# Layer 3 of a four-layer model: the four scan directions summed with tokens on the partitions, with D * x and layer norm done there, and group norm's deviation moved to ScalarE

## The chip, the cores and the metric

The kernel runs on one core of one Trainium2 chip, in float32. The metric is device microseconds from the first to the last instruction of one launch that computes all four layers for 16 images of 192 channels and 32 x 32 pixels.

## The reference, cut to what matters

Each layer adds its output to its input, after a group norm of 32 groups:

```python
x = x + _L0(_gn(x), ...)     # an mLSTM block and a 3x3 convolution
x = x + _L1(_gn(x), ...)     # a Mamba block
x = x + _L2(_gn(x), ...)     # a depthwise convolution and a batch norm
x = x + _L3(_gn(x), ...)     # a Mamba block that scans the image in four directions

def _gn(v, G=32, eps=1e-5):  # mean and variance over a group's channels and pixels
    return ((g - m) / jnp.sqrt(s + eps)).reshape(v.shape)
```

What the change touches in layer 3 (DI = 384, 16 states, L = 32 * 32 tokens):

```python
x_in, z = (xz[:, :DI], xz[:, DI:])
xc = silu(_dwconv(x_in, conv_w, conv_b, ((1, 2), (1, 2))))
x_hw, x_wh = rows_in_order(xc), columns_in_order(xc)
xs = stack([x_hw, x_wh, x_hw[..., ::-1], x_wh[..., ::-1]])     # four directions
def step(h, inp):                                              # for each direction
    h = h * exp(dt_t[..., None] * A) + (dt_t * u_t)[..., None] * B_t
    y = sum(h * C_t, axis=-1)
ys = scan(step) + Ds * xs
y = ys[0] + inv_wh(ys[1]) + ys[2][..., ::-1] + inv_wh(ys[3][..., ::-1])
y = (y - mean(y)) / sqrt(var(y) + 1e-5) * ln_g + ln_b          # over the 384 channels
y = y * silu(z)
g_out = y @ W_out + b_out
return wts[0] * g_out + wts[1] * l_out                         # l_out: a convolution branch
```

`inv_wh` turns a sequence that ran down the columns back into row order.

## The kernel before, in words

Layer 0 works in chunks of 128 tokens; layers 1 and 2 run together; layer 3 has a loop of its own, `scan_run`. The pieces are tied together by queues written out by hand: `Side` holds generators with a start and an end, counted in steps, and `tick` runs each one's share of pieces between the pieces of the main loop. A scheduler then settles the order on each engine, and every engine takes its instructions strictly in order.

A **step** of layer 3 is one of 16 states of one **unit**, and a unit is one direction over one half (512 tokens) of one image, so an image has 8 units and 128 steps. The directions come in the order k = 0, 2 (rows, forward and backward), then 1, 3 (columns). In a step ScalarE computes three decays (`da`, L986) and scales three inputs (`xbt`, L966); TensorE turns the inputs so that channels lie on partitions (`xb`, L994 and L997); VectorE runs three scans of 128x512 (`h`, L1010); GpSimd multiplies all three by C (L1017, one instruction of 128x1536; a small `carry` copy, L1016, in every other unit); and TensorE adds the result to `y` in PSUM, turned so that tokens lie on partitions (L1028), two steps later. `y` has a single buffer: when a unit's sixteenth state is in, `layer3_sum` reads it out (L1466 by ScalarE for the first direction of a pair, L1468 by VectorE to add the second), and the next unit's first L1028 waits for that. SyncE's queue loads a row of C per step (`cb`, L968).

Everything else of an image is side work at fixed steps `at` (counted from the image's first):

- steps 2 to 8: `layer3_columns` of the image before. Six blocks of four transposes (L1064) bring the sum of the two column directions back to channels on partitions, and VectorE adds each to `v` with a strided pattern (L1490).
- steps 8 to 36: `layer3_tail` of the image before. For each half, layer norm over the channels, which lie on partitions: matmuls with a matrix of 1/384 for mean and variance (L377, L385), differences and products by VectorE (L379, L389), squares, logarithm and exponential by ScalarE (L384, L386, L387); silu of z between two loads of function tables (L1283, L1284); gain and bias (L1656); the product with silu(z) by GpSimd (L1660). Then the output projection (L1668), and VectorE adds the residual (L1671).
- steps 36.5 to 45: `layer3_front` of the next image, with `group_norm`: statistics by VectorE, a matmul over the groups, epsilon by VectorE (L367), the power -0.5 by GpSimd (L309), then the normalization by VectorE (L1545).
- steps 45 to 78: the next image's convolution branch (`layer3_local`) and z (`layer3_z`, matmuls L1594, whose input is read along the image's rows).
- steps 66 to 74: `layer3_rows`: the sum of the two row directions back to channels on partitions, with D * x (L1477).
- steps 78 to 112: the next image's `layer3_xc` (projection and a 4x4 depthwise convolution, L1171, then silu).
- steps 114 to 125: `prep` of the next image's first unit. Each other unit's `prep` (its dt, B and C rows, L887 to L937) runs 14 to 3 steps before the unit; column units read `xc` with a stride of 32 elements in L887.

After the last step the last image's columns and tail run alone. `group_norm` serves all four layers.

Of the kernel before, what the change touches and what calls it, by code (L numbers as in the profile page):

```python
# [22 lines left out]
W = 32  # L23
# [5 lines left out]
EPS = 1e-5  # L29
# [67 lines left out]
def lay_out(a):  # L97
# [26 lines left out]
    p128.add("3conv_r", taps(a["L3_conv_conv_w"].reshape(DI, 4, 4)))  # L124
    for n in ("b_in", "conv_b", "ln_g", "ln_b"):
        p128.vec("3" + n, a["L3_conv_" + n])
    p128.vec("3Ds", a["L3_conv_Ds"].T)
    p128.vec("3A_log", a["L3_conv_A_log"].transpose(1, 0, 2))

    def in96(w):  # L130
        return w.reshape(2, HP, -1).transpose(1, 0, 2)
# [13 lines left out]
    def x_rows(w):  # L145
# [35 lines left out]
        "w3_dt": pair(dt_rows, a["L3_conv_dt_proj_w"], a["L3_conv_dt_proj_b"]).reshape(-1, 2 * DI),  # L181
        "w3_out": in128(a["L3_conv_W_out"]),
        "w3_pw": in96(a["L3_conv_pw_w"].T),
    }
    arrays = {k: np.ascontiguousarray(v) for k, v in arrays.items()}
    return arrays, p96.at, p128.at, const.at, const0.at
# [88 lines left out]
class Program:  # L275
# [68 lines left out]
    def group_norm(self, pool, psum, x):  # L344

        nc = self.nc
        st = pool.tile([HP, 2, 2, 6], F32, name="gnst")
        mv = pool.tile([HP, 2, 2], F32, name="gnmv")
        for m in range(2):
            for i, h in enumerate(halves()):  # L350
                nc.vector.bn_stats(st[:, m, i], x[:, m, h])
            nc.vector.bn_aggr(mv[:, m], st[:, m].rearrange("p a b -> p (a b)"))
            yield 1
        ps = psum.tile([128, 512], F32, name="mm")
        nc.tensor.matmul(ps[:HP, :2], self.k("group", HP), mv[:, :, 0], start=True, stop=True)
        mean = pool.tile([HP, 2], F32, name="gnmean")
        nc.vector.tensor_copy(mean, ps[:HP, :2])
        d = pool.tile([HP, 2], F32, name="gnd")
        nc.vector.tensor_tensor(d, mv[:, :, 0], mean, SUB)
        q = pool.tile([HP, 2], F32, name="gnq")  # L360
        nc.vector.tensor_tensor(q, d, d, MUL)
        nc.vector.tensor_tensor(q, q, mv[:, :, 1], ADD)
        yield 1
        ps = psum.tile([128, 512], F32, name="mm")
        nc.tensor.matmul(ps[:HP, :2], self.k("group", HP), q, start=True, stop=True)
        r = pool.tile([HP, 2], F32, name="gnr")
        nc.vector.tensor_scalar(r, ps[:HP, :2], EPS, None, ADD)  # L367
        self.pow_mhalf(r)
        yield 1
        return mean, r, d  # L370

# [1005 lines left out]
    def layer3(self):  # L1377
        tc = self.tc
        with (
# [53 lines left out]
            for b in range(self.nb):  # L1433
                at = 8 * NS * b
                if b:
                    side.add("columns", self.layer3_columns(b - 1, bp, psum), at + 2, at + 8)
                    side.add("tail", self.layer3_tail(b - 1, bp, psum), at + 8, at + 36)
                else:
                    side.add("local", self.layer3_local(0, sp, bp, psum), 3, 33)
                    side.add("z", self.layer3_z(0, bp, psum), 5, 35)  # L1440
                for j in range(1, 8):
                    side.add("prep", prep(units[8 * b + j]), at + 16 * j - 14, at + 16 * j - 3)
                if b + 1 < self.nb:
                    side.add("front", self.layer3_front(b + 1, sp, bp, dp, psum), at + 36.5, at + 45)
                    side.add("local", self.layer3_local(b + 1, sp, bp, psum), at + 45, at + 77)
                    side.add("z", self.layer3_z(b + 1, bp, psum), at + 46, at + 78)
                side.add("rows", self.layer3_rows(b, bp, psum), at + 66, at + 74)
                if b + 1 < self.nb:
                    side.add("xc", self.layer3_xc(b + 1, bp, dp, psum), at + 78, at + 112)
                if b + 1 < self.nb:  # L1450
                    side.add("prep", prep(units[8 * b + 8]), at + 114, at + 125)
# [1 line left out]
            finish(self.layer3_xc(0, bp, dp, psum))  # L1453
            finish(prep(units[0]))
            self.scan_run(units, side, bp, psum)
            finish(self.layer3_columns(self.nb - 1, bp, psum))
            finish(self.layer3_tail(self.nb - 1, bp, psum))

    def layer3_sum(self, u, y, bp):

        im = self.image[u.b]
        if u.k < 2 and u.half == 0:
            im["sum"] = bp.tile([128, 8, DI], F32, name="ysum", bufs=1)
        t = im["sum"][:, 4 * u.half : 4 * u.half + 4].rearrange("p c d -> p (c d)")
        if u.k < 2:
            self.nc.scalar.copy(t, y)  # L1466
        else:
            self.nc.vector.tensor_tensor(t, t, y, ADD)  # L1468

    def layer3_rows(self, b, bp, psum):  # L1470

        im = self.image[b]
        v = im["v"] = bp.tile([128, 3, S], F32, name="v", bufs=1)
        for t in range(3):
            for i, h in enumerate(halves()):
                ps = self.untranspose(im["sum"][:, 4 * i : 4 * i + 4], t, psum)
                self.nc.vector.scalar_tensor_tensor(  # L1477
                    v[:, t, h], im["xc"][:, t, h], self.ds[:, t : t + 1], ps, MUL, ADD
                )
                yield  # L1480

    def layer3_columns(self, b, bp, psum):

        im = self.image[b]
        v = im["v"].rearrange("p t (h w) -> p t w h", w=W)
        for t in range(3):
            for i in range(2):
                ps = self.untranspose(im["sum"][:, 4 * i : 4 * i + 4], t, psum)
                o = v[:, t, 16 * i : 16 * i + 16]
                self.nc.vector.tensor_tensor(o, o, ps.rearrange("p (w h) -> p w h", h=W), ADD)  # L1490
                yield

    def layer3_weights(self, wp, bp, dp):
        nc = self.nc
# [10 lines left out]
        self.ds = wp.tile([128, 3], F32, name="ds")  # L1505
        nc.vector.tensor_reduce(self.ds, self.v128("3Ds", 0, 12).rearrange("p (t k) -> p t k", k=4), AX.X, ADD)

        self.t_conv = dp.tile([3, 128, 16, 32], F32, name="t_conv3", bufs=1)
        for t in range(3):
# [77 lines left out]
    def layer3_z(self, b, bp, psum):  # L1587

        nc = self.nc
        for i in range(2):  # L1590
            for t in range(3):
                ps = psum.tile([128, 512], F32, name="mm")
                for m in range(2):
                    nc.tensor.matmul(  # L1594
                        ps, self.w_in[:, m, DI + t * 128 : DI + (t + 1) * 128],
                        self.xpad[:, m, 1 + 16 * i : 17 + 16 * i, 1 : 1 + W], start=m == 0, stop=m == 1,
                    )
                z = bp.tile([128, 512], F32, name="xt")
# [42 lines left out]
        self.silu(xc)  # L1641
        yield

    def layer3_tail(self, b, bp, psum):

        nc = self.nc
        im = self.image.pop(b)
        wts, v = im["wts"], im["v"]
        for i, h in enumerate(halves()):
            sz = bp.tile([128, 3, 512], F32, name="tmp", bufs=1)  # L1650
            nc.sync.dma_start(sz, self.sz3[b % 2, i])
            vs = [v[:, t, h] for t in range(3)]
            yield from self.layer_norm(bp, psum, vs, vs, self.k("ones384"), 128, 512)
            self.silu(sz)
            for t in range(3):
                nc.scalar.activation(  # L1656
                    v[:, t, h], v[:, t, h], AF.Identity, bias=self.v128("3ln_b", t), scale=self.v128("3ln_g", t)
                )
                yield 0.4
            nc.gpsimd.tensor_tensor(v[:, :, h], v[:, :, h], sz, MUL)  # L1660
            yield 0.4
        for m in range(2):
            for h in halves():
                x = bp.tile([HP, 512], F32, name="xt")
                nc.sync.dma_start(x, self.x3[b, :, m, h])
                ps = psum.tile([128, 512], F32, name="mm")
                for t in range(3):
                    nc.tensor.matmul(  # L1668
                        ps[:HP], self.w_out[:, t, m * HP : (m + 1) * HP], v[:, t, h], start=t == 0, stop=t == 2
                    )  # L1670
                nc.vector.scalar_tensor_tensor(x, ps[:HP], wts[:, 0:1], x, MUL, ADD)  # L1671
                nc.sync.dma_start(self.out[b, m * HP : (m + 1) * HP, h], x)
                yield 2.6

    def router(self, sp, psum, d, r):

# [34 lines left out]
```

## Time and profile before

| | us |
|---|---|
| median of 3 runs | 17365.07 (17350.37 to 17365.62) |
| the profiled execution's own time | 17403.5 |
| its span, first to last instruction | 17401.7 |
| layer 3's scan loop, from the first scan to the last | 7767 to 17335 |
| one image of it | 601 to 604 |

| engine | busy us of the span |
|---|---|
| PE (matmul) | 15749.6 (91%) |
| DVE (VectorE) | 13122.0 (75%) |
| ACT (ScalarE) | 11873.6 (68%) |
| POOL (GpSimd) | 11450.8 (66%) |

A group's line gives its source line, engine, operation, tile, shape and count, then the busy time of the group and the mean duration of one in ns. In a table by stretch each number pair is busy us and a count. A matmul of float32 leaves two records, a transpose one. A busy PE includes the time in which a matmul drains.

### The profile page before, as it was taken

The numbers are of one execution on the slowest core, as the hardware profiler recorded it, in microseconds if no ns is written. First come the engines' busy times: TensorE is split into PE (matmuls) and PEld (weight loads), VectorE is DVE, ScalarE is ACT, GpSimd is POOL, SyncE is SP. The second block draws the span as 40 slices with busy tenths as digits, with TensorE's granted clock in tenths as the row PEclk, the third lists the DMA queues.
The fourth block names the chain that finished last, engine by engine and source line by source line (L and its number), as shares of the span: only waits on it lengthen the run. The fifth ranks groups of instructions, "written<-read, shape, count | busy, mean of one in ns | idle before, by whom it ended". The sixth has DMA issues, their size and how long they took to land. (4 is left out here: it accounts for less than half of the span.)

```text
span 17401.7 us, 263068 instructions
## 1 busy us (share of the span) xinstructions
PE 15749.6 (91%) x99452; PEld 11013.2 (63%) x99452; DVE 13122.0 (75%) x14859; ACT 11873.6 (68%) x19637; POOL 11450.8 (66%) x5555
## 2 busy tenths in 40 slices
PE   8998988888988899979899999999999999999998
PEld 4444444435555555547777777777777777777777
DVE  4444444437777777749889888888888888888888
ACT  3222322327666666648888888888888888888888
POOL 3333333425555555538788788888878888888888
PEclk8889998989999999989999999999999999999999
DMA  1111111123333343433333333323333333333332
GB/s 51 42 40 44 44 43 44 47 63 107 114 110 110 113 118 116 118 99 103 90 99 107 93 96 101 107 83 99 107 98 92 99 108 88 96 105 102 88 98 67
DMA packets 890141, 1544.65 MB, mean 89 GB/s; under 512 B 83472, under 2 KB 314653, under 8 KB 879530
## 3 DMA queue, kind: packets, MB, share of 16 engines
q1 hardware_dynamic: 888874, 1527.81, 30.3%
q8 instruction: 788, 12.91, 0.3%
q14 instruction: 479, 3.92, 0.1%
HBM read 1284.22 MB, written 243.27 MB: 88 GB/s over the span
## 5 line engine op out<-in xcount | busy, mean ns | idle before, releaser
L1017 POOL TENSOR_TENSOR h<-h,cb 128x1536 f32<-128x1536 f32 x2560 | 8872.8, 3469 | 1432.0 <-DVE h L1010 902.9
L986 ACT ACTIVATE da<-dt,neg_a 128x512 f32<-128x512 f32 x7680 | 5267.0, 714 | 1752.0 <-DVE h L1010 1687.3
L1010 DVE TENSOR_TENSOR_SCAN h<-da,carry,xb 128x512 f32<-128x512 f32 x3840 | 4652.4, 1262 | 657.1 <-PE xb L997 596.2
L1028 PE MATMUL y<-const,h 128*128 128x128 f32 x30720 | 4717.9, 276 | 128.3 <-DVE ysum L1468 54.0
L1010 DVE TENSOR_TENSOR_SCAN h<-da,xb 128x512 f32<-128x512 f32 x3840 | 4440.6, 1202 | 388.7 <-PE xb L997 270.7
L994 PE MATMUL xb<-const,xbt 128*128 128x128 f32 x23040 | 4074.6, 282 | 422.5 <-DVE h L1010 269.3
L966 ACT ACTIVATE xbt<-ut,bt 128x384 f32<-128x384 f32 x7680 | 4174.4, 603 | 246.4 <-PE xb L994 244.3
L994 PEld LDWEIGHTS xb<-const,xbt 128*128 128x128 f32 x23040 | 2757.2, 143 | 1815.5 <-issue 643.8
L1028 PEld LDWEIGHTS y<-const,h 128*128 128x128 f32 x30720 | 3684.9, 143 | 322.8 <-issue 265.4
L997 PE MATMUL xb<-diag,ut 128*128 128x128 f32 x15360 | 3016.4, 279 | 0.0
L997 PEld LDWEIGHTS xb<-diag,ut 128*128 128x128 f32 x15360 | 2383.5, 195 | 63.1 <-issue 63.1
L830 POOL TENSOR_TENSOR hs<-h,mhm 128x384 f32<-128x384 f32 x128 | 108.5, 848 | 1685.1 <-DVE den L835 1290.5
L1016 POOL COPY carry<-h 128x3 f32<-128x3 f32 x1280 | 250.5, 196 | 1220.1 <-DVE h L1010 964.7
L976 POOL TENSOR_TENSOR diag<-const,bt 128x512 f32<-128x512 f32 x640 | 680.8, 1064 | 550.5 <-PE xb L997 362.1
L705 POOL TENSOR_TENSOR e<-e,const 128x1536 f32<-128x1536 f32 x128 | 439.9, 3437 | 288.9 <-DMA e<-row 273.0
L520 PE MATMUL conv<-ya,w_conv 128*64 128x512 f32 (+1 forms) x1152 | 543.9, 656 | 66.1 <-DMA ya<-yrows 62.2
L916 PE MATMUL mm<-dbl,w_dt 45*128 45x512 f32 x960 | 532.8, 639 | 33.6 <-DVE v L1490 16.2
L711 ACT ACTIVATE e<-e 128x1536 f32<-128x1536 f32 x128 | 189.7, 1482 | 417.7 <-POOL e L706 417.4
L854 DVE TENSOR_TENSOR ht<-sz,mm 128x384 f32<-128x384 f32 x128 | 70.7, 552 | 519.5 <-PE mm L851 519.5
L1171 PE MATMUL mm<-rep,t_dw 96*32 96x512 f32 x2304 | 433.5, 614 | 23.5 <-DMA rep<-xr 17.3
L779 PEld LDWEIGHTS num<-v,p 128*128 128x128 f32 x3072 | 389.3, 201 | 102.2 <-issue 77.9
L920 DVE SCALAR_TENSOR_TENSOR dt<-lnsq,mm 128x512 f32<-128x512 f32 x480 | 322.0, 671 | 171.9 <-ACT lnsq L919 171.9
(272 smaller groups left out, 17910.1 us busy)
## 6 DMA issues: line engine op xcount, KB each, us to landing
cb<-row SPq DMA_DIRECT2D x2560, 256.0 KB
rep<-xr SPq DMA_DIRECT2D x384, 331.0 KB
e<-row SPq DMA_DIRECT2D x128, 768.0 KB
rep<-xin SPq DMA_DIRECT2D x384, 256.0 KB
rep<-xr SPq DMA_DIRECT2D x384, 228.8 KB
x<-x SPq DMA_DIRECT2D x48, 768.0 KB
xr<-xin SPq DMA_DIRECT2D x48, 612.5 KB
xr<-xpad SPq DMA_DIRECT2D x32, 867.0 KB
```

The source lines that it names most:

```text
L520: nc.tensor.matmul(o, self.w_c2[:k, t, c0 : c0 + o.shape[0]], src[:k, r0 : r0 + 16, dx : dx + W], start=t == 0, stop=t == 14, skip_group_c ...
L705: nc.gpsimd.tensor_tensor(k.e, k.e, self.k0("mask")[:, None, :].to_broadcast([128, NH, 128]), ADD)
L916: nc.tensor.matmul(ps, w_dt[:, t * 128 : (t + 1) * 128], dbl, start=True, stop=True)
L966: nc.scalar.activation(t[:, c], u.ut[:, c], AF.Copy, scale=u.bt[:, c, n : n + 1])
L976: nc.gpsimd.tensor_tensor(d, ident[:, None, :].to_broadcast([128, 4, 128]), u.bt[:, 3, n : n + 4][:, :, None].to_broadcast([128, 4, 128]), ...
L986: nc.scalar.activation(da[i, t], u.dt[:, t], AF.Exp, scale=u.neg_a(t, n))
L994: in_order(nc.tensor.transpose(xb[i, t][:, c * 128 : (c + 1) * 128], xbt[i][:, c, t * 128 : (t + 1) * 128], ident))
L997: in_order(nc.tensor.matmul(xb[i, t][:, 384:], u.ut[:, 3, t * 128 : (t + 1) * 128], u.diag[n // 4][:, n % 4], start=True, stop=True, skip_ ...
L1010: nc.vector.tensor_tensor_scan(hv, dv, xv, 0.0 if first else u.carry_in[:, n, t : t + 1], MUL, ADD)
L1017: nc.gpsimd.tensor_tensor(h[i], h[i], u.c.pop(n)[:, None, :].to_broadcast([128, 3, 512]), MUL)
L1028: in_order(nc.tensor.matmul(u.y[:, j], h[i][:, t, c * 128 : (c + 1) * 128], ident, is_transpose=True, start=n == 0 and j % 4 == 0, stop=n ...
L1171: self.nc.tensor.matmul(ps[32 * g : 32 * g + 32], blocks[:, g * side + r], seen, start=r == 0, stop=r == side - 1, skip_group_check=True,)
```

## The change

`layer3_columns`, `layer3_rows` and `layer3_tail` go. In their place:

- `layer3_turn` writes the row directions' sum (tokens on partitions) to DRAM and reads it back in the columns' order into the same tile, in eight DMAs. The column directions are then added to it by VectorE, so that of eight units only the first two are copied by ScalarE.
- `layer3_skip` adds D * x by GpSimd, in two products and two sums of 128x1536, using `xtok`, which by then holds x in the columns' order.
- `layer3_norm` does layer norm along the free dimension: statistics by VectorE, logarithm and exponential of 4 columns by ScalarE, and one VectorE instruction of 128x384 per block of tokens; then the transposes, with gain and bias applied by ScalarE as it reads PSUM, and the product with silu(z) by GpSimd. The second half of an image is done at steps 115 to 127, the first half at steps 2 to 14 of the next image.
- `layer3_out` loads and stores the residual whole, one buffer instead of two, and VectorE writes it in row order with a strided pattern.
- z is computed in the columns' order: its matmuls read their input down the image's columns.
- `group_norm` takes epsilon, logarithm and exponential by ScalarE instead of VectorE's sum and GpSimd's power, in all layers.

```diff
@@ group_norm
-        nc.vector.tensor_scalar(r, ps[:HP, :2], EPS, None, ADD)
-        self.pow_mhalf(r)
+        nc.scalar.activation(r, ps[:HP, :2], AF.Ln, bias=self.k("eps", HP))
+        nc.scalar.activation(r, r, AF.Exp, scale=-0.5)
@@ layer3
-                    side.add("columns", self.layer3_columns(b - 1, bp, psum), at + 2, at + 8)
-                    side.add("tail", self.layer3_tail(b - 1, bp, psum), at + 8, at + 36)
+                    side.add("norm", self.layer3_norm(b - 1, 0, sp, bp, psum), at + 2, at + 14)
+                    side.add("out", self.layer3_out(b - 1, bp, psum), at + 14.5, at + 35)
...
-                side.add("rows", self.layer3_rows(b, bp, psum), at + 66, at + 74)
+                side.add("turn", self.layer3_turn(b, dp), at + 66.5, at + 68)
+                side.add("skip", self.layer3_skip(b, bp), at + 80, at + 110)
+                side.add("norm", self.layer3_norm(b, 1, sp, bp, psum), at + 115, at + 127)
...
-            finish(self.layer3_columns(self.nb - 1, bp, psum))
-            finish(self.layer3_tail(self.nb - 1, bp, psum))
+            finish(self.layer3_norm(self.nb - 1, 0, sp, bp, psum))
+            finish(self.layer3_out(self.nb - 1, bp, psum))
@@ layer3_sum
-        if u.k < 2:
+        if u.k == 0:
             self.nc.scalar.copy(t, y)
         else:
             self.nc.vector.tensor_tensor(t, t, y, ADD)
+    def layer3_turn(self, b, dp):
+        y = self.image[b]["sum"]
+        rows = dp.tile([S, DI], F32, name="yrows", bufs=2)
+        self.nc.sync.dma_start(rows.rearrange("(c p) d -> p c d", p=128), y)
+        yield Wait(0.7)
+        for c in range(8):
+            self.nc.sync.dma_start(y[:, c], rows.rearrange("(h w) d -> w h d", w=W)[4 * c : 4 * c + 4])
...
+    def layer3_skip(self, b, bp):
...
+        for i in range(2):
...
+            nc.gpsimd.tensor_tensor(dx, im["xtok"][:, h], self.ds[:, None, :].to_broadcast([128, 4, DI]), MUL)
+            yield 1
+            nc.gpsimd.tensor_tensor(im["sum"][:, h], im["sum"][:, h], dx, ADD)
+            yield 1
+    def layer3_norm(self, b, i, sp, bp, psum):
...
+        for c in range(4):
+            nc.vector.bn_stats(st[:, c], y[:, c])
+            nc.vector.bn_aggr(mv[:, c], st[:, c])
+            yield 1
+        r = sp.tile([128, 4], F32, name="lnr")
+        nc.scalar.activation(r, mv[:, :, 1], AF.Ln, bias=self.k("eps"))
+        nc.scalar.activation(r, r, AF.Exp, scale=-0.5)
+        yield 1
+        for c in range(4):
+            nc.vector.tensor_scalar(y[:, c], y[:, c], mv[:, c, 0:1], r[:, c : c + 1], SUB, MUL)
+            yield 0.8
+        self.silu(z)
+        yield 3
         for t in range(3):
+            ps = self.untranspose(y, t, psum)
+            nc.scalar.activation(
+                v[:, t], ps, AF.Identity, bias=self.v128("3ln_b", t), scale=self.v128("3ln_g", t)
+            )
+            yield 1.2
+        nc.gpsimd.tensor_tensor(v, v, z, MUL)
+        yield 1
@@ layer3_z
-                        self.xpad[:, m, 1 + 16 * i : 17 + 16 * i, 1 : 1 + W], start=m == 0, stop=m == 1,
+                        self.xpad[:, m, 1 : 1 + W, 1 + 16 * i : 17 + 16 * i].rearrange("p h w -> p w h"),
+                        start=m == 0, stop=m == 1,
                     )
-                z = bp.tile([128, 512], F32, name="xt")
+                z = bp.tile([128, 512], F32, name="z", bufs=1)
@@ layer3_tail -> layer3_out
-            yield from self.layer_norm(bp, psum, vs, vs, self.k("ones384"), 128, 512)
-            self.silu(sz)
...
-            nc.gpsimd.tensor_tensor(v[:, :, h], v[:, :, h], sz, MUL)
...
+            x = bp.tile([HP, S], F32, name="xt", bufs=1)
+            nc.sync.dma_start(x, self.x3[b, :, m])
+            yield Wait(1.5)
+            for i, h in enumerate(halves()):
...
-                nc.vector.scalar_tensor_tensor(x, ps[:HP], wts[:, 0:1], x, MUL, ADD)
-                nc.sync.dma_start(self.out[b, m * HP : (m + 1) * HP, h], x)
+                o = x.rearrange("p (h w) -> p w h", w=W)[:, 16 * i : 16 * i + 16]
+                nc.vector.scalar_tensor_tensor(
+                    o, ps[:HP].rearrange("p (w h) -> p w h", h=W), wts[:, 0:1], o, MUL, ADD
+                )
+                yield 1
+            nc.sync.dma_start(self.out[b, m * HP : (m + 1) * HP], x)
```

More of the change, by code (lines that the diff above doesn't have):

```diff
@@ L126, in lay_out @@
         p128.vec("3" + n, a["L3_conv_" + n])
-    p128.vec("3Ds", a["L3_conv_Ds"].T)
     p128.vec("3A_log", a["L3_conv_A_log"].transpose(1, 0, 2))
@@ L183, in lay_out @@
         "w3_pw": in96(a["L3_conv_pw_w"].T),
+        "d3": a["L3_conv_Ds"].reshape(1, 4 * DI),
     }
@@ L1455, in layer3 @@
             self.scan_run(units, side, bp, psum)
-            finish(self.layer3_columns(self.nb - 1, bp, psum))
-            finish(self.layer3_tail(self.nb - 1, bp, psum))
+            finish(self.layer3_norm(self.nb - 1, 0, sp, bp, psum))
+            finish(self.layer3_out(self.nb - 1, bp, psum))
     def layer3_sum(self, u, y, bp):
         im = self.image[u.b]
-        if u.k < 2 and u.half == 0:
+        if u.k == 0 and u.half == 0:
             im["sum"] = bp.tile([128, 8, DI], F32, name="ysum", bufs=1)
         t = im["sum"][:, 4 * u.half : 4 * u.half + 4].rearrange("p c d -> p (c d)")
-        if u.k < 2:
+        if u.k == 0:
             self.nc.scalar.copy(t, y)
@@ L1468, in layer3_sum @@
             self.nc.vector.tensor_tensor(t, t, y, ADD)
-    def layer3_rows(self, b, bp, psum):
-        im = self.image[b]
-        v = im["v"] = bp.tile([128, 3, S], F32, name="v", bufs=1)
-        for t in range(3):
[L1475 to L1491, printed above, removed]
+    def layer3_turn(self, b, dp):
[5 more added lines that the diff above has]
+            self.nc.sync.dma_start(y[:, c], rows.rearrange("(h w) d -> w h d", w=W)[4 * c : 4 * c + 4])
+            if c % 2:
+                yield 1
@@ new lines, in layer3_skip @@
+    def layer3_skip(self, b, bp):
+        nc = self.nc
+        im = self.image[b]
+        for i in range(2):
+            h = slice(4 * i, 4 * i + 4)
+            dx = bp.tile([128, 3, 512], F32, name="tmp", bufs=1).rearrange("p a b -> p (a b)")
+            dx = dx.rearrange("p (c d) -> p c d", c=4)
+            nc.gpsimd.tensor_tensor(dx, im["xtok"][:, h], self.ds[:, None, :].to_broadcast([128, 4, DI]), MUL)
+            yield 1
+            nc.gpsimd.tensor_tensor(im["sum"][:, h], im["sum"][:, h], dx, ADD)
+            yield 1
@@ new lines, in layer3_norm @@
+    def layer3_norm(self, b, i, sp, bp, psum):
+        nc = self.nc
+        im = self.image[b]
+        if i:
+            im["v"] = bp.tile([128, 3, S], F32, name="v", bufs=1)
+        v = im["v"][:, :, 512 * i : 512 * i + 512]
+        y = im["sum"][:, 4 * i : 4 * i + 4]
+        z = bp.tile([128, 3, 512], F32, name="tmp", bufs=1)
+        nc.sync.dma_start(z, self.sz3[b % 2, i])
+        st = sp.tile([128, 4, 6], F32, name="lnst")
+        mv = sp.tile([128, 4, 2], F32, name="lnmv")
+        for c in range(4):
[11 more added lines that the diff above has]
+        yield 3
+        for t in range(3):
+            ps = self.untranspose(y, t, psum)
[5 more added lines that the diff above has]
+        yield 1
@@ L1503, in layer3_weights @@
         nc.vector.tensor_scalar(self.neg_a, self.neg_a, -1.0, None, MUL)
-        self.ds = wp.tile([128, 3], F32, name="ds")
-        nc.vector.tensor_reduce(self.ds, self.v128("3Ds", 0, 12).rearrange("p (t k) -> p t k", k=4), AX.X, ADD)
+        d = bp.tile([128, 3, 512], F32, name="tmp", bufs=1).rearrange("p a b -> p (a b)")
+        nc.sync.dma_start(d, self.ins["d3"].partition_broadcast(128))
+        self.ds = wp.tile([128, DI], F32, name="ds")
+        nc.vector.tensor_reduce(self.ds, d.rearrange("p (k d) -> p d k", k=4), AX.X, ADD)
         self.t_conv = dp.tile([3, 128, 16, 32], F32, name="t_conv3", bufs=1)
@@ L1642, in layer3_xc, with layer3_out @@
         yield
-    def layer3_tail(self, b, bp, psum):
+    def layer3_out(self, b, bp, psum):
         nc = self.nc
@@ L1648, in layer3_tail @@
         wts, v = im["wts"], im["v"]
[L1649 to L1652, printed above, removed]
-            yield from self.layer_norm(bp, psum, vs, vs, self.k("ones384"), 128, 512)
-            self.silu(sz)
[L1655 to L1661, printed above, removed]
         for m in range(2):
-            for h in halves():
-                x = bp.tile([HP, 512], F32, name="xt")
-                nc.sync.dma_start(x, self.x3[b, :, m, h])
+            x = bp.tile([HP, S], F32, name="xt", bufs=1)
+            nc.sync.dma_start(x, self.x3[b, :, m])
+            yield Wait(1.5)
+            for i, h in enumerate(halves()):
                 ps = psum.tile([128, 512], F32, name="mm")
@@ L1670, in layer3_tail @@
                     )
-                nc.vector.scalar_tensor_tensor(x, ps[:HP], wts[:, 0:1], x, MUL, ADD)
-                nc.sync.dma_start(self.out[b, m * HP : (m + 1) * HP, h], x)
-                yield 2.6
+                o = x.rearrange("p (h w) -> p w h", w=W)[:, 16 * i : 16 * i + 16]
+                nc.vector.scalar_tensor_tensor(
+                    o, ps[:HP].rearrange("p (w h) -> p w h", h=W), wts[:, 0:1], o, MUL, ADD
+                )
+                yield 1
+            nc.sync.dma_start(self.out[b, m * HP : (m + 1) * HP], x)
     def router(self, sp, psum, d, r):
```

## The prediction

> **What bounds the kernel now.** I began with the busy shares and went to the side work's own stretches, since a share is a mean over stages. The image whose loop starts at 11381.8 is cut at steps 2, 14, 36, 46, 80, 112 and 2 (601.1 us in all). The table of windows gives for each stretch its length, then PE, PEld, DVE, ACT and POOL busy:
>
> ```profile
> 11388.50:11454.30 65.80, 57.87 (x408) 46.55 (x407) 56.37 (x58) 53.85 (x93) 48.28 (x28) 0.97 0.25 67
> 11454.30:11562.00 107.70, 94.39 (x656) 74.68 (x657) 92.51 (x90) 98.47 (x160) 90.67 (x38) 0.98 0.28 80
> 11562.00:11610.00 48.00, 37.12 (x261) 33.66 (x260) 46.11 (x48) 36.42 (x63) 37.45 (x22) 0.86 0.27 85
> 11610.00:11777.00 167.00, 162.30 (x1153) 123.83 (x1153) 148.82 (x147) 135.59 (x234) 131.22 (x63) 1.00 0.36 103
> 11777.00:11921.00 144.00, 143.09 (x1123) 108.42 (x1122) 123.93 (x116) 127.64 (x213) 124.62 (x59) 1.00 0.45 136
> 11921.00:11989.60 68.60, 63.51 (x506) 56.54 (x505) 66.27 (x61) 64.24 (x115) 62.16 (x23) 0.98 0.27 77
> ```
>
> Call them A1, A2, B, C, D, E. No engine bounds the image alone. C and D belong to TensorE (97% and 99%); B and E to VectorE (96%, 97%), in E with ScalarE at 94% close behind. In A1 and A2 nothing is above 91%: waits cost there. Who waits in layer 3 (total us, times, longest), and what stands in for the change's costs:
>
> ```profile
> PE mm L1668 <- POOL v L1660: 77.0, 17, 10.3
> PE y L1028 <- DVE ysum L1468: 54.0, 32, 2.7
> PE y L1028 <- ACT ysum L1466: 21.2, 30, 1.1
> PE y L1028 <- POOL h L1017: 16.9, 27, 1.9
> ```
> ```profile
> 11635.40:11641.30 5.90, 5.48 (x6) 0.91 (x6) 1.00 0.62 170
> 11914.80:11917.90 3.10, 2.83 (x6) 0.93 (x6) 1.00 0.06 19
> ```
> ```profile
> L1541 DVE SCALAR_TENSOR_TENSOR x<-tmp,x x64: 656/730/3481, 7651.5 to 16396.7; 96x512 f32<-96x512 f32 x64
> ```
> ```profile
> L377 PE MATMUL mm<-v,const 128*128 128x512 f32 x192 | 90.4, 593 | 0.3 <-DVE v L1490 0.3
> L385 PE MATMUL mm<-lnsq,const 128*128 128x512 f32 x192 | 108.9, 649 | 43.3 <-ACT lnsq L384 22.5 <-ACT xtok L932 20.8
> L1064 PE MATMUL mm<-const,ysum 128*128 128x128 f32 x1152 | 186.2, 287 | 33.7 <-ACT o L1257 18.5 <-DVE dt L920 6.7 <-DVE o L1140 3.8
> ```
>
> The first: the projection stands in TensorE's queue behind GpSimd's product, 4.8 us per image, and all turns behind it. The second is L887 alone, six records reading `xc` by columns (stride 32), then by rows: 5.48 against 2.83, so a strided record costs 0.44 us more. The third: an instruction with two operands in SBUF takes 0.73 us or up to 3.48.
>
> **What the Trainium skill says.** "SBUF — State Buffer", Door 1: The DMA port swizzle, says SBUF is read in lines of 16 bytes and that accesses which go to a new line each time pay; L887 agrees (0.47 to 0.91 us per record). The same page, Who interferes with whom, says that a VectorE instruction with two SBUF inputs, or in a two-port mode such as tensor_scalar from SBUF, and a GpSimd instruction exclude each other for the whole instruction. L1541 agrees, and L379, with one operand in PSUM, stays at 660 to 689 ns. "ScalarE: Activation LUTs", Table sets: the hidden batching unit, has logarithm and exponential in one set; L386 and L387 follow each other with no load between, so the new pairs need none.
>
> **The change part by part**, per image.
>
> *A1 and A2* (173.5 us; PE 152.3, DVE 148.9, ACT 152.3, POOL 139.0). TensorE loses layer norm's matmuls, (90.4+108.9)/16 = 12.5, and 24 transposes of the columns for 12 of the norm: 768 of L1064's 1152 are layer 3's, 186.2x768/1152/16 = 7.8 for 48, so 3.9 less 1.9. PE 137.8. VectorE loses six L1490 (1.135 each, 6.8) and twelve L379/L389 (0.62, 7.5); it gains four statistics of 384 (L351's 0.667x384/512 = 0.5) with their aggregation (0.18), four normalizations (L577's 512 take 0.546 and L1545's 1024 take 0.80, so about 0.48), and four residuals with a strided output (1.135 as L1490 instead of 0.74): 4.6 + 1.6. The four normalizations are tensor_scalar from SBUF, open to GpSimd's lock; L1541's mean of 1.568 against 0.68 unblocked prices it at 0.9 each (0 to 1.7, half a GpSimd product): 3.6. DVE 144.4. ScalarE loses squares (60.2/16 = 3.8), L386/L387 (2.5), L1656 (4.8) and one of two silus (1.28+1.49+1.28 = 4.05), and gains three reads of PSUM (0.68) and two short ones (0.21 as L839): 12.7 less, 139.6. GpSimd loses one product, 3.45. The busiest falls from 152.3 to 144.4; at the present ratio of 1.14 that is 164.5, and the wait for L1660 (4.8) should go, since the norm ends at step 14 and the projection starts 1.5 steps later or more: 160. I take -13 (-8 to -19).
>
> *B.* VectorE's wait for the power, L1545 <- L309, is 23.7 us over the stage, 1.5 per image. ScalarE takes the pair over; the decays queue behind it. -1.5 (-2.5 to +1: L1545 meets GpSimd's lock, 1.7).
>
> *C.* z's 24 records now read down the columns (stride 34): 24x0.44 = +10.6. The rows' 24 transposes go: -3.9. PE 162.3 becomes 169.0, at 1.03 173.9: +7 (+4 to +10). VectorE's six L1477 (4.4) cost nothing now and free nothing. SyncE gets nine DMAs, the first behind VectorE's sum, the reads behind the write; the C rows queue behind them, but are loaded two steps ahead, as beside the eight reads of `xtok` today. z's single buffer waits for its store; the pieces are over two steps apart. 0 for both; without that cover a few us.
>
> *D* (TensorE at 99%). Two sums go from ScalarE to VectorE, and the next unit's L1028 waits 54.0/32 = 1.7 instead of 21.2/30 = 0.7: +2. GpSimd gets four instructions of 3.45, 13.8, and is then busy 138 of 144. In the order of the changed program one stands at step 73 (in C), two side by side at 82, one at 98. Queued behind them are the products by C, and behind those L1028, with all turns. Today's 32 L1660 are such inserts, and L1028's whole wait for GpSimd is 16.9/32 = 0.5 each: +2; the pair (6.9 us against a cover of about one step) may cost more. +5 in all for D (+2 to +13).
>
> *E.* A norm falls in: VectorE +4.6 and 3.6 of lock, ScalarE +6.5 (4.05 silu, 0.4, 2.0), TensorE +1.9, GpSimd +3.45. ScalarE alone comes to 70.7, VectorE to 74.5, against 68.6. +7 (+3 to +10).
>
> *Sum.* A and B occur 15 times in the loop, C, D, E 16 times: 15x(-14.5) + 16x19 = +87.
>
> *The end.* From the last sum (17341.4) to the end the kernel takes 60.3 us. One norm instead of all columns and both halves: sum 1.7, statistics 2.7, pair 0.5, silu with loads 4.05 (normalization beside it), three reads 2.0, product 3.4, then 24 records of projection, 13.5 (18 take 10.4 today; the first six are slower there too), residual 1.1 and store 3.2: 32, with gaps 33. -27 (-20 to -32).
>
> *Layers 0 to 2.* Group norm makes TensorE wait 96.8 us in layer 0 (L377 <- L543, 15 times). ScalarE's pair stands behind L839/L840, which wait for VectorE behind GpSimd's lock, and the normalization then waits for the same GpSimd instructions: only the power's 0.69 goes, 15 times. GpSimd no longer waits in its queue for L367 (143.9 us, 21 times), ScalarE may instead. -15 (-90 to +40).
>
> Net +45 on the profiled 17403.5, whose own run lies 38 over the median. On the median: **17410**.
>
> **The rivals.**
>
> *A's waits are worth more than their share (faster).* The chain silu, L1656, L1660, L1668 halts every engine: for L1668 the longest wait is 10.3. If A falls by 20 to its busiest engine plus 6%, and C, D, E cost TensorE's share only (+6.7, +2, +3), it is 15x(-21.5) + 16x11.7 - 42 = -177: 17190. With C to E as forecast it decides from -17.5 per image in A and B. For it: 21 us of A lie above its busiest engine. Against: E has no engine below 90%. A milder form, with the middle of both sets, gives 17300.
>
> *TensorE alone sets the period (faster).* Then only 12.5+7.8-3.9-10.6 = 5.8 per image counts: -93-42, 17230. Against: PE is at 93% over the image, and B and E are not its own.
>
> *GpSimd and its lock become the bound (slower).* If the two products at 82 are not covered (+13 in D) and each normalization waits half a product (1.7; A -10, E +9): 15x(-11.5) + 16x29 - 42 = +250: 17615. For it: L1541's 3481 ns. It decides where inserts cost over 1 us each.
>
> That the change doesn't do what it says: its order has 24 transposes fewer per image, no L377/L385 in layer 3, and the strided z. Excluded.
>
> **How the numbers follow.** 0.2% (35 us) is about what a measurement of this kernel can tell. The forecast's own band, 17340 to 17480, holds 0.52: 0.36 above 17400, 0.16 within 0.2%. The faster rivals have 0.35 together, GpSimd 0.13. So faster 0.35, same 0.16, slower 0.49. Leaving out the far ends, the range is 17230 to 17590.
>
> **What would show it.** Right: z's records near 0.9 us; no wait of the projection for GpSimd; C longer by about 7 and E by 5 to 9, A1+A2 near 160; normalizations with a mean well above their minimum; L1028's wait for sums near 54+32 = 86 us. Wrong: C unchanged (strided z at 0.47), A below 155, or L1028 waiting over 60 us for GpSimd.

## The result, and the profile after

The changed kernel takes **17430.21 us** (median of 5 runs, 17424.42 to 17438.88) against 17363.56 for the kernel before: a ratio of **1.0040**, 95% interval 1.0026 to 1.0055, slower by 67 us. In the profiled executions the spans are 17422.6 and 17401.7.

The same windows as before, of the same image (now starting at 11332.5), cut at the same steps: length, then PE, PEld, DVE, ACT and POOL busy, TensorE's granted clock, DMA share, GB/s.

```profile
11339.14:11407.08 67.94, 56.56 (x373) 46.16 (x372) 54.27 (x57) 55.82 (x96) 56.00 (x31) 0.86 0.26 73
11407.08:11503.01 95.93, 88.36 (x649) 72.68 (x648) 92.76 (x87) 84.20 (x142) 78.54 (x32) 0.99 0.26 79
11503.01:11548.35 45.34, 38.56 (x287) 33.93 (x285) 42.65 (x45) 37.65 (x68) 41.64 (x26) 0.92 0.31 95
11548.35:11723.25 174.90, 170.53 (x1094) 122.45 (x1093) 141.65 (x136) 132.55 (x228) 129.59 (x60) 0.97 0.37 109
11723.25:11869.37 146.12, 144.71 (x1118) 107.89 (x1117) 126.64 (x118) 125.39 (x211) 134.95 (x63) 1.00 0.45 140
11869.37:11952.54 83.17, 70.81 (x541) 61.37 (x540) 75.93 (x74) 74.00 (x128) 67.10 (x24) 0.96 0.24 73
```

A2 is shorter, C and E are longer. One image has jitter, so here are the means of the same stretches over the 14 middle images, from the scans' starts (E up to step 128; the image also has steps 0 and 1, 6.7 us in both):

| us per image | A1 | A2 | B | C | D | E | image |
|---|---|---|---|---|---|---|---|
| before | 65.6 | 107.9 | 50.4 | 163.6 | 143.8 | 64.0 | 602.0 |
| after | 67.2 | 96.4 | 45.4 | 173.1 | 145.6 | 76.0 | 610.3 |
| TensorE at half clock, before | 3.2 | 7.3 | 10.7 | 2.9 | 0.0 | 2.0 | 26.1 |
| the same, after | 14.7 | 1.9 | 5.6 | 6.9 | 0.0 | 9.5 | 38.5 |

The lower rows come from the trace's record of the granted clock: in layer 3 TensorE is at full or at half clock, and a spell at half clock lasts about 3.4 us, or a multiple of that.

The first image of the loop went from 606.9 to 648.6 us (+42), and the last from 533.2 to 554.3 (+21). From the first scan of layer 3 to the last it is 9568.2 before and 9747.3 after (+179); what follows the last scan, 65.8 and 43.7 (-22); the time ahead of the loop, 7767.7 and 7631.6 (-136).

TensorE's waits in layer 3 (total us, times, longest):

```profile
PE xb L994 <- DVE h L1010: 324.5, 362, 3.0
PE xb L994 <- ACT xbt L966: 84.8, 127, 4.0
PE mm L1697 <- POOL v L1528: 79.4, 15, 5.4
PE y L1028 <- POOL h L1017: 62.9, 66, 9.5
PE y L1028 <- DVE ysum L1470: 50.7, 50, 2.5
```

The projection still waits for GpSimd's product, L1697 where it was L1668, with the same total as before. The matmuls of z, L1594 before and L1634 after (ns: minimum, median, maximum):

```profile
L1594 PE MATMUL mm<-xpad,w_in x384: 592/592/1066, 7798.3 to 16558.5; 96*128 96x512 f32 x192
```
```profile
L1634 PE MATMUL mm<-xpad,w_in x384: 1112/1134/1278, 7662.3 to 16562.1; 96*128 96x512 f32 x192
```

And what VectorE does on `ysum` after: the normalizations L1518 have a minimum of 445 ns and a maximum of 2754, while statistics and sums are even.

```profile
L1510 DVE BATCH_NORM_STATS2 lnst<-ysum x128: 519/531/560, 8206.4 to 17389.5; 128x6 f32<-128x384 f32 x128
L1518 DVE TENSOR_SCALAR ysum<-ysum,lnmv,lnr x128: 445/472/2754, 8219.2 to 17392.0; 128x384 f32<-128x384 f32 x128
L1470 DVE TENSOR_TENSOR ysum<-ysum,y x96: 1722/1728/1754, 7889.5 to 17386.2; 128x1536 f32<-128x1536 f32 x96
```

### The profile page after: what moved, and what is told of

The parts are those of the page before. It is cut to its first block, busy times and chain, and to the rows that moved or that the text cites. A ratio compares the mean times of both kernels' runs of the same rounds, so it can differ in the third digit from the quotient of the medians.

```text
span 17422.6 us, 261823 instructions
## 1 busy us (share of the span) xinstructions
PE 15795.4 (91%) x98684; PEld 10986.1 (63%) x98684; DVE 13099.5 (75%) x14827; ACT 11787.9 (68%) x19639; POOL 11641.4 (67%) x5555
## 4 chain that ended last, share of the span: by engine, by line
PE 33%; DVE 8%; POOL 6%; issue 5%; ACT 3%; DMA 0%; SPq 0%; POOLq 0%; DVEq 0%; ACTq 0%
PE y L1028 10%; PE xb L994 8%; DVE h L1010 6%; PE xb L997 5%; POOL h L1017 5%; PE mm L1171 3%; PE mm L1634 2%; PE mm L916 2%; PE mm L887 1%; ACT xbt L966 1%; ACT da L986 1%; PE mm L1655 1%; PE mm L936 1%; PE mm L1619 1%; PE mm L1697 1%
## 5 line engine op out<-in xcount | busy, mean ns | idle before, releaser
L1017 POOL TENSOR_TENSOR h<-h,cb 128x1536 f32<-128x1536 f32 x2560 | 8880.8, 3472 | 1559.7 <-DVE h L1010 1094.9
L1028 PE MATMUL y<-const,h 128*128 128x128 f32 x30720 | 4763.8, 278 | 149.3 <-POOL h L1017 64.9
L1028 PEld LDWEIGHTS y<-const,h 128*128 128x128 f32 x30720 | 3727.5, 145 | 382.4 <-issue 292.6
L997 PE MATMUL xb<-diag,ut 128*128 128x128 f32 x15360 | 3052.5, 281 | 0.0
L1171 PE MATMUL mm<-rep,taps 128*32 128x512 f32 x3072 | 435.7, 606 | 26.9 <-DMA rep<-xr 15.7
L854 DVE TENSOR_TENSOR ht<-sz,mm 128x384 f32<-128x384 f32 x128 | 70.6, 552 | 497.8 <-PE mm L851 497.7
```

The costliest lines, as they stand in the source:

```text
L997: in_order(nc.tensor.matmul(xb[i, t][:, 384:], u.ut[:, 3, t * 128 : (t + 1) * 128], u.diag[n // 4][:, n % 4], start=True, stop=True, skip_ ...
L1017: nc.gpsimd.tensor_tensor(h[i], h[i], u.c.pop(n)[:, None, :].to_broadcast([128, 3, 512]), MUL)
L1028: in_order(nc.tensor.matmul(u.y[:, j], h[i][:, t, c * 128 : (c + 1) * 128], ident, is_transpose=True, start=n == 0 and j % 4 == 0, stop=n ...
L1171: self.nc.tensor.matmul(ps[32 * g : 32 * g + 32], blocks[:, g * side + r], seen, start=r == 0, stop=r == side - 1, skip_group_check=True,)
```

## The experiments

Every ratio is to the kernel before, from runs on the same chip, with its 95% interval. The changed kernel itself is 1.0040 in the first measurement and 1.0045 (1.0028 to 1.0062) when it was run again.

**e9_after_again.** The changed kernel itself, beside e5, e6 and e7.

> The changed kernel itself, on the same chip as the three beside it, so that they can be compared with it as well as with the kernel before. Every theory: a ratio of 1.003 to 1.0055 to the kernel before, as measured first.

17417.22 us, 1.0045. The stretches repeat to within 0.5 us.

**e1_gn_only and e2_layer3_only.** The change in its two parts.

```diff
 # e1: the kernel before, with group_norm of the changed one
-        nc.vector.tensor_scalar(r, ps[:HP, :2], EPS, None, ADD)
-        self.pow_mhalf(r)
+        nc.scalar.activation(r, ps[:HP, :2], AF.Ln, bias=self.k("eps", HP))
+        nc.scalar.activation(r, r, AF.Exp, scale=-0.5)
 # e2: the changed kernel, with group_norm of the one before (the reverse)
```

> The kernel before with one part of the change: group norm's logarithm and exponential by ScalarE, in all layers. Theory: the 136 us by which layer 3's first scan starts earlier in the changed kernel (7631.6 instead of 7767.7) all come from this edit, 5 us per image in layer 0 and 3.6 in layers 1 and 2, so this kernel takes 17364 - 135 = about 17230 and its layer 3 loop stays at 602 per image. Rival, the prediction's own step: the edit is worth 15 us (17350), and the early start comes from another order in the queues that only the whole change brings.

> The changed kernel with group norm as before, so layer 3's new arrangement alone. Theory: layer 3 alone costs the loop's +178 less 22 at the end, so 17364 + 155 to 200 = 17520 to 17565, with its first scan near 7768. Rival: if the two parts are not additive (the prediction's -15 for group norm), it stands at 17445.

e1: 17247.16 us, 0.9949 (0.9934 to 0.9963). e2: 17534.9, 1.0118 (1.0101 to 1.0135). So the two lines of group norm are worth 88 us (0.51% of 17334, that chip's median) and the rest of the change costs over twice that. Together they would give 1.0067; the changed kernel, at 1.0040 to 1.0045, is a little better than its parts. The waits ahead of layer 3 show where group norm's gain lies, first e2's, with the power on GpSimd, then e1's:

```profile
POOL gnr L309 <- DVE gnr L367: 129.9, 19, 40.1
...
PE mm L377 <- DVE x L543: 98.9, 15, 8.1
```
```profile
PE mm L377 <- DVE x L543: 55.6, 17, 4.9
```

TensorE's wait for the normalized image in layer 0 falls by 43 us, half the gain, and GpSimd doesn't stand in its queue for VectorE any more. e2 also corrects the profile of before: with the same group norm ahead of layer 3, its first scan there is at 7713.6, where the profiled run of before had 7767.7. So some 54 of the 136 us were that run's own; 41 of them had built up by the end of layer 0, in which that run was at half clock for 85 us longer.

**e3_z_runs.** z's matmuls read runs of 16 pixels of a row, and VectorE turns the block as it leaves PSUM.

```diff
-                        self.xpad[:, m, 1 : 1 + W, 1 + 16 * i : 17 + 16 * i].rearrange("p h w -> p w h"),
+                        self.xpad[:, m, 1 : 1 + W, 1 + 16 * i : 17 + 16 * i],
...
-                nc.vector.tensor_scalar(z, ps, self.v128("3b_in", t + 3), None, ADD)
+                nc.vector.tensor_scalar(
+                    z.rearrange("p (w h) -> p w h", h=W), ps.rearrange("p (h w) -> p w h", w=16),
+                    self.v128("3b_in", t + 3), None, ADD,
+                )
```

> The changed kernel with z's matmuls reading runs of 16 pixels along the rows, and VectorE turning the block while it takes it out of PSUM (strided read and write there). Theory: the strided read by TensorE sets steps 46 to 80, so z's records go from 1.13 us back to about 0.6, steps 46 to 80 from 173 to about 163, 16 images: -160, 17270. VectorE's six instructions become 0.3 to 0.5 us longer, 2 to 3 us per image, beside TensorE's work. Rival: VectorE's wait and its longer eviction in the same steps take the place, less than -60.

17229.88 us, **0.9938** (0.9923 to 0.9953): 1% less than the changed kernel. C falls from 173.1 to 162.2, below its length before; the first image from 648.6 to 620.8. The matmul, VectorE's eviction, and the window of C in the same image as above:

```profile
L1634 PE MATMUL mm<-xpad,w_in x384: 626/628/1201, 7688.9 to 16390.1; 96*128 96x512 f32 x192
```
```profile
L1639 DVE TENSOR_SCALAR z<-mm,p x96: 735/750/753, 7691.0 to 16390.8; 128x512 f32<-128x512 f32 x96
```
```profile
11485.50:11645.60 160.10, 155.46 (x1095) 117.32 (x1093) 140.37 (x137) 132.00 (x228) 128.92 (x60) 1.00 0.38 118
```

Runs of 16 elements are nearly as fast as whole rows, 628 ns against 592, and turning the block on the way out costs VectorE nothing (a mean of 748 ns a block in the changed kernel, a median of 750 here). The strided read alone costs more than the change loses.

**e4_out_later.** The output projection starts four and a half steps later.

```diff
-                    side.add("out", self.layer3_out(b - 1, bp, psum), at + 14.5, at + 35)
+                    side.add("out", self.layer3_out(b - 1, bp, psum), at + 19, at + 35)
```

> The changed kernel with the output projection started at step 19 instead of 14.5, so that in TensorE's queue its first matmul stands at step 20 instead of 13. Theory: TensorE's wait for GpSimd's product with silu(z) (79.4 us, 15 times) stops everything at step 13, and it goes: step 13 falls from 9.7 to about 4.5, -5 per image, 17430 - 75 = 17355. Rival: TensorE's wait is filled by ScalarE's and GpSimd's backlog, which bind these steps anyway; the wait goes but the time stays, 17415 to 17440.

17513.44 us, 1.0101 (1.0086 to 1.0116): slower still, which neither theory had. Its waits in layer 3:

```profile
PE xb L994 <- ACT xbt L966: 108.5, 112, 4.4
PE y L1028 <- POOL h L1017: 101.2, 111, 10.0
...
PE mm L1716 <- DVE wide L1715: 28.7, 14, 2.4
PE mm L916 <- DVE dt L920: 24.4, 28, 1.5
```

The wait for L1528 is gone (79 us), but A1 + A2 is 163.5 as after: the sums over its two halves only changed places (61.7 + 101.8 for 67.2 + 96.4), and TensorE waits longer for L1017, `xbt` and `wide` instead. B and C became 2.3 and 2.9 us longer, with 9.3 and 14.6 us at half clock for 5.6 and 6.9. The edit also crowds the projection into steps 19 to 35; the wait was not taken away in any other way.

**e12_placeholder.** One more matmul takes the early place of L1697 in TensorE's order.

```diff
                 ps = psum.tile([128, 512], F32, name="mm")
+                for _ in range(m == 0 and i == 0):
+                    nc.tensor.matmul(
+                        ps[:HP], self.w_out[:, 0, :HP], self.w_out.rearrange("p t d -> p (t d)")[:, :512], start=True, stop=True
+                    )
```

> The changed kernel with one more matmul, of weights with weights, ahead of layer3_out's first (its result is overwritten). It takes the place in TensorE's order, in the middle of step 13's matmuls, at which the first L1697 stood, and that one comes a step later; nothing else moves. Theory: the wait for GpSimd's product (75 to 79 us in all) shrinks by a step's length to 1 or 2 us an image, and the 6.4 us at half clock in steps 13 and 14 go with it: steps 2 to 36 get 5 to 8 us shorter, 75 to 120 us in all: a ratio of 0.998 to 1.000. Rival: as when layer3_out began at step 19, TensorE runs ahead and waits for GpSimd's and ScalarE's work a few steps later instead: a ratio of 1.003 to 1.005.

17430.35 us, 1.0047 (1.003 to 1.0064): the rival's number, but by another way. The wait hardly shrank:

```profile
PE mm L1701 <- POOL v L1528: 62.9, 14, 4.5
```

Step 13 still takes 9.4 us (9.7), so the first real one is still waited for there. This run doesn't tell what the wait is worth. In e4 it is gone, and A1 + A2 is no shorter.

**e5_no_skip.** D * x by GpSimd is left out.

```diff
-                side.add("skip", self.layer3_skip(b, bp), at + 80, at + 110)
```

> The changed kernel without layer3_skip: D * x is left out of layer 3, so GpSimd loses four instructions of 3.5 us in steps 80 to 112 of each image. Theory: TensorE bounds that stretch (144 of 145.6 us busy after, 142.8 of 143.8 before) and the inserts fit into GpSimd's slack, so the stretch goes back by 1 to 2 us an image and the first image by some 10 us (its L1491 stood early in GpSimd's queue and waited for a transfer): about 30 us less in all, a ratio to the kernel before of 1.002. Rival: GpSimd, 93% busy in that stretch, has become its bound, and most of the 14 us comes off each image: a ratio of 0.993 or less.

17362.4 us, 1.0012 (1.0005 to 1.0018), 55 us less than the changed kernel beside it (e9): the theory forecast about 30. Against e9, a middle image takes 2.2 us less (D falls by 0.7, C by 1.7: the first insert stands at the end of C), the first 11 and the last 16. So half of the 55 us lies in two images. In the first, all four inserts stand side by side at steps 74 to 77. The insert that waits 5.6 us for the transfer of `xtok` is the last image's, at step 46; my expectation put it in the first. And the last image has no next image's work beside which GpSimd's could pass unnoticed. L1028's wait for GpSimd is back near its size before (16.9):

```profile
PE y L1028 <- POOL h L1017: 21.1, 27, 7.2
```

GpSimd was 93% busy in D, and still 14 us of its work in a middle image cost 2 to 3.

**e6_two_inputs.** The normalization as an instruction with two input tensors.

```diff
-            nc.vector.tensor_scalar(y[:, c], y[:, c], mv[:, c, 0:1], r[:, c : c + 1], SUB, MUL)
+            nc.vector.scalar_tensor_tensor(
+                y[:, c], y[:, c], mv[:, c, 0:1], r[:, c : c + 1].to_broadcast([128, DI]), SUB, MUL
+            )
```

> The changed kernel with the normalization (L1518) as SCALAR_TENSOR_TENSOR, whose second input is the reciprocal deviation broadcast along the columns; the same engine, place and arithmetic. Theory: VectorE's one-input form waits for GpSimd's running instruction, its two-input forms don't (their records are even: L1470 1722 to 1728 ns), and the waits, 7.5 us an image over the 445 ns minimum, stand ahead of the scans in VectorE's queue, where TensorE waits for them. The mean of L1518 falls from about 1.4 us in these stretches to about 0.6 us, steps 112 to 128 get 3 us shorter and steps 2 to 14 3 us: some 80 us in all, a ratio of 0.9995. Rival: the waits are covered, or the new form waits as well: a ratio of 1.004 as for the changed kernel itself.

17429.61 us, 1.0055 (1.0038 to 1.0072): no gain. The new form waits as the old one did:

```profile
L1518 DVE SCALAR_TENSOR_TENSOR ysum<-ysum,lnmv,lnr x128: 580/610/3160, 8229.3 to 17382.6; 128x384 f32<-128x384 f32 x128
```

My premise was a misreading: L1470 has two inputs, but its second, `y`, is in PSUM. The Trainium skill ("SBUF — State Buffer", Who interferes with whom) says that two SBUF inputs contend with a GpSimd instruction that reads SBUF; `ysum` and the broadcast column both lie in SBUF, and the maximum of 3160 ns agrees.

**e10_no_normalize.** The eight normalizations of an image are left out.

```diff
         for c in range(4):
-            nc.vector.tensor_scalar(y[:, c], y[:, c], mv[:, c, 0:1], r[:, c : c + 1], SUB, MUL)
             yield 0.8
```

> The changed kernel without the eight normalizations of an image (L1518, one subtraction and multiplication of 128x384 each, left out; the statistics stay). They took 10.7 us of VectorE an image, 7.1 of them waits over the 445 ns minimum, ahead of the scans in VectorE's queue. Theory: these waits are what makes steps 112 to 128 12 us and steps 2 to 14 1.6 us longer, together with the half clock that TensorE gets after a wait; without them steps 112 to 128 take 66 to 69 us and steps 2 to 14 61 to 63, 12 us an image and some 180 us in all: a ratio of 0.994. Rival: the stretch is long for the other parts of layer3_norm, its twelve transposes, its activations and TensorE's half clock; then under 4 us an image: a ratio of 1.001 to 1.003.

17268.08 us, **0.9957** (0.9942 to 0.9972): 0.8 to 0.9% less than the changed kernel. E falls from 76.0 to 70.7 and A1 from 67.2 to 61.4; the other stretches stay within 0.3. In E that is less than the 7 to 10 us that the theory gave; A1 is as it had it. The two windows, A1 and E, of the same image:

```profile
11282.46:11344.24 61.78, 50.97 (x373) 43.48 (x372) 48.43 (x53) 55.80 (x96) 55.57 (x31) 0.93 0.27 81
...
11803.02:11879.90 76.88, 69.08 (x541) 60.56 (x540) 71.41 (x71) 73.21 (x128) 66.83 (x24) 0.98 0.26 79
```

How a wait of VectorE spreads is seen in the changed kernel's timeline, E of the next image (start, length, engine; the bracket is idle time and what ended it), first VectorE, then GpSimd, then TensorE:

```profile
12509.51 1.27 DVE L1010 TENSOR_TENSOR_SCAN h<-da,carry,xb 128x512 f32<-128x512 f32 x1
12510.71 2.44 DVE L1518 TENSOR_SCALAR ysum<-ysum,lnmv,lnr 128x384 f32<-128x384 f32 x1
12513.07 1.27 DVE L1010 TENSOR_TENSOR_SCAN h<-da,carry,xb 128x512 f32<-128x512 f32 x1
```
```profile
12509.35 3.58 POOL L1017 TENSOR_TENSOR h<-h,cb 128x1536 f32<-128x1536 f32 x1 [1.54 <-issue]
```
```profile
12507.21 0.60 PE L1028 MATMUL y<-const,h 128*128 128x128 f32 x4
12509.27 0.55 PE L994 MATMUL xb<-const,xbt 128*128 128x128 f32 x3 [1.46 <-DVE h L1010]
...
12511.96 1.06 PE L1028 MATMUL y<-const,h 128*128 128x128 f32 x4
12514.39 0.90 PE L994 MATMUL xb<-const,xbt 128*128 128x128 f32 x3 [1.37 <-DVE h L1010]
```

L1518 ends 0.2 us after L1017 (at 12513.15, 12512.93); the next scan is two microseconds late, TensorE has nothing to turn in the meantime, and then does the same four matmuls in 1.06 us instead of 0.60. In the means, steps 118 and 119 fall from 5.4 and 6.3 us to 3.5 and 3.5 without L1518, and steps 5 and 6 from 6.9 and 6.5 to 3.5 and 3.9.

**e7_no_silu.** The silu of z in the norm is left out.

```diff
-        self.silu(z)
```

> The changed kernel without the silu of z in layer3_norm (left out; z multiplies as it is), so ScalarE loses twice an image a block of 4.05 us, a table load of 1.28, the 1536-column activation of 1.49 and the load back of 1.28. Theory: this block delays the chunks' da and xbt by its own length in a step of 3.5 us, TensorE waits and then runs at half clock for one window; each block costs some 4 us, 8 us an image, 120 us in all: a ratio of 0.997. Rival: the delay in steps 118 to 121 and 5 to 9 is VectorE's lock waits, and ScalarE catches up in the same time: a ratio of 1.003 to 1.004.

17389.67 us, 1.0031 (1.0023 to 1.0038): 0.14% less than the changed kernel, near the rival. A1 falls by 4.9 (step 8 from 8.2 to 4.2 us), as the theory has it for one block; E falls by 0.7 only, perhaps since L1518's wait holds the same steps; no run leaves out both. A2 and C are 1.5 and 1.9 longer, C with 10.5 us at half clock for 6.9.

**e11_runs_act_norm.** e3, with the normalization by ScalarE.

```diff
+        neg = sp.tile([128, 4], F32, name="lnneg")
+        nc.gpsimd.tensor_tensor(neg, mv[:, :, 0], r, MUL)
+        nc.gpsimd.tensor_scalar(neg, neg, -1.0, None, MUL)
+        yield 1
         for c in range(4):
-            nc.vector.tensor_scalar(y[:, c], y[:, c], mv[:, c, 0:1], r[:, c : c + 1], SUB, MUL)
+            nc.scalar.activation(y[:, c], y[:, c], AF.Identity, bias=neg[:, c : c + 1], scale=r[:, c : c + 1])
             yield 0.8
```

> The version with z read in runs of 16 pixels (ratio 0.9938), with the normalization moved to ScalarE: Identity with the reciprocal deviation as scale and minus mean times it as bias, the bias by two small GpSimd instructions. Theory: ScalarE doesn't wait for GpSimd's lock, so the waits of 7 us an image go, and the 4 x 0.6 us a half that ScalarE gains find room in its 0.83 to 0.88 busy share: 5 us an image, some 80 us: a ratio of 0.989. Rival: da and xbt come from ScalarE one chunk at a time, so what it gains delays TensorE just as the silu block did (5 us an image in steps 2 to 14): a ratio of 0.993 to 0.997.

17111.52 us (17100.54 to 17117.25), **0.9865** (0.985 to 0.988): faster than both kernels, and by more than the theory said. The image takes 588.5 us: C 162.3 as in e3, E 70.6 and A1 63.1, nearly what leaving L1518 out gave. ScalarE's form is longer than VectorE's unhindered one (697 ns each; 445), but even (688 to 710 ns), and E and A1 are 4.6 and 4.2 us shorter than in e3:

```profile
L1522 ACT ACTIVATE ysum<-ysum,lnneg,lnr 128x384 f32<-128x384 f32 x128 | 88.8, 697 | 3.7 <-POOL lnneg L1519 3.7
```

## Why the prediction was right, and which of its steps were not

The direction and the size came out: 17410 was forecast and 17430 measured, in the forecast's own band, on the side that had the highest chance. But the size owes much to luck. The loop cost +179 where the sum had +87, and the layers ahead of it gained about 70 where it had 15: two misses in opposite directions, which nearly cancelled. Of the loop's miss, 53 us lie in the 14 middle images (+8.3 each, forecast +4.5), 23 in the first and 17 in the last.

- **C, +7: +9.5; the mechanism held.** TensorE's busy time became 169.0 as worked out, and the stretch 173.1 (173.9), but in part by luck. The sum began at one image with 162.3 us busy in 167.0, where the means of before are 159.1 and 163.6; and the price of a strided record was low: 0.44 us was taken from L887's stride of 32, and z pays 0.54 (1134 - 592), 2.4 us more for 24 records. e3 shows that the stride is the cost: -10.9.
- **E, +7: +12.0, outside its range of +3 to +10.** VectorE's work was sized rightly: 75.9 us busy in the window above, 74.5 forecast, and e10 prices L1518 at 5.3 us in E, 4 x (0.48 + 0.9) = 5.5 in the working. The step that failed is that the stretch would stay as close to its busiest engine as before. It was 97% of it and became 91%: what VectorE takes while it waits comes at once to the next scans, TensorE runs dry, and then has 9.5 us at half clock instead of 2.0. Of the 12 us, 5.3 are L1518 by e10; the other 6.6, the transposes, activations, statistics and silu, were not separated. Silu alone gave 0.7, with L1518 still there.
- **A, -13: -9.9; the step "the wait for L1660 should go" failed.** The scheduler put the first L1697 in the middle of step 13 on TensorE, ahead of its due time, and the wait kept its total (77.0 and 79.4). e4, which takes it away by starting the projection later, leaves A at 163.5, so this wait alone is not why A missed -13. The work taken from TensorE, VectorE and ScalarE is what is left to explain the shorter A; no run varied it alone. L1518's lock wait was priced right, 0.9 us each for a measured 1340 - 445 ns over layer 3, and e10's 5.8 us in A1 agrees with 5.5.
- **B, -1.5: -5.0.** Group norm's part was sized rightly: e1 has B at 49.0 for 50.4, and the changed kernel 45.4 for 46.8 in e2, 1.4 both times. The other 3.6 us come with the rest of the change, for which the sum had nothing; B has 3.4 us less at half clock in e2 than before, and no run parts it further.
- **D, +5: +1.8.** L1028's wait for sums did not grow to 86 us; it shrank from 75.2 to 50.7. Its wait for GpSimd did pass the 60 us named as a sign of error, 62.9, but none of it lies in D of the 14 middle images: 9.5 us are in C of the first image and 31 in the last. e5 prices the inserts at 55 us in all, half of it in these two images.
- **The first image, +19 in the sum (C, D and E): +42.** By e3 28 of it is z, which falls into this image twice: 24 strided records in A, for the image itself, that the sum left out, and 24 in C for the next. By e5 11 are the four inserts of D * x in a row.
- **The last image, +4.5 in the sum: +21.** It has no z and no next image's front, so its C and D are short (135.2 and 122.5 us before) and became 150.1 and 131.5. L1028's wait for GpSimd rose from 6 to 31 us there, and e5 takes 16 of the 21 us back. The sum used the middle images' terms for it, whose D has 144.0 us of TensorE's work in 145.6 beside GpSimd's 135.0.
- **The end, -27: -22.**
- **Layers 0 to 2, -15: about -70** (the 88 us of e1 and e2 less 16 times 1.4 in B). Here the argument itself failed. It allowed only the power's 0.69 us to go, since ScalarE's pair would stand in a queue. In layer 0 the way from the group matmul (L365) to the end of the second normalization went from between 11 and 12 us to between 8.3 and 9.1 an image: both hand-overs to and from GpSimd with their queues went, not the power's own time alone. e1 and e2 show 43 us of it as TensorE's wait; the rest, in layers 1 and 2, wasn't followed wait by wait. The profile had it: 143.9 us of GpSimd's wait for L367 stood in the working, and was given to ScalarE.
- **The base.** The sum was made against 17403.5 and carried to the median by taking off 38. e2 shows where the profiled run was slow, ahead of layer 3 (some 54 us); a stretch that the change hardly touches can carry the whole difference.

Of the rivals, "A's waits are worth more" fails: the wait kept its total, and in e4, where it went, A was no shorter. "TensorE alone" fails by E. "GpSimd and its lock" had the right mechanism in the normalizations, though not at 1.7 us each, and in the inserts for the first and last image, though not for the pair at step 82 of the others.

## What to carry to other kernels

A strided read by a matmul weighs most where TensorE has least room, here in C. Reading runs of 16 elements and turning the block in the instruction that takes it out of PSUM took 628 ns a record instead of 1134, at no cost to VectorE. Where GpSimd runs most of the time, keep instructions that wait for its lock out of the engine whose results TensorE awaits next: four such instructions of 0.45 us, with 0.9 of wait each, cost 5 to 6 us a time, and moving them to ScalarE gave back 4.2 to 4.6 of it. Price the first and the last round of a loop on their own: what covers a cost in the middle can be missing there. When a wait of TensorE disappears and the time doesn't, look for the next wait and for its clock before looking for another cause.

## What the runs showed that I had not expected

**A strided matmul can lower TensorE's clock while it is busy.** "TensorE: Matmul & The Clock Gate", Part 1: The HAM clock gate, in the Trainium skill says that the clock is halved after an idle window of about 3.4 us and comes back after a busy one; the spells' length here agrees (of 129 in the scan loop, 85 last 3.4 us and 31 twice that). But of the 34 spells in C of the changed kernel, 30 begin within 7 us of a record of L1634, with TensorE busy for the whole 3.4 us ahead. Before, C has 12 spells, in e3 13; most of these follow some idle time. It comes on top of the record's own 0.54 us, and its amount changes from kernel to kernel (6.9 us of C after, 14.6 in e4, with the same z). e3 shows that the spells go with the stride; that such reads count as low activity is my inference.

**Short waits are enough for half clock.** In the timeline above, a spell at half clock begins at 12511.01. In the 3.4 us ahead of it TensorE had waited 1.46 and 0.45 us, 1.9 us together, and neither wait is as long as a window; the wait of 1.37 us falls within the spell, which lasts 6.8 us.
